# Ten of sixteen decayed sums moved from a matmul to VectorE's scan between two turns, and three weighings of the last pairs moved from TensorE to VectorE

## The chip, the cores and the metric

The kernel runs on one core of a Trainium2 chip. The metric is the device time of one execution in microseconds. The kernel before took 465.46 us (median of three runs, 465.07 to 465.91).

## The reference, cut to what matters

Four gated blocks in a row work on `x`, 32 sequences of 128 tokens with 256 features, with a context `ctx_1024` of the same shape. All arithmetic is in float32. Only the first and the end of the last are touched by the change.

```python
# block 1: a decayed sum of the squared context, times the normed x
def _L0_xattn_ref(q, k, v):            # q = layernorm(x), k = v = ctx_1024
    kv = swapaxes(k * v, 0, 1)
    def step(r, kv_t):
        r = 0.9 * r + kv_t             # along the 128 tokens of a sequence
        return (r, r)
    _, rs = jax.lax.scan(step, r0, kv)
    return q * swapaxes(rs, 0, 1)

x = x + tanh(g_xattn[0]) * _L0_xattn_ref(layernorm(x), ctx_1024, ctx_1024)
x = x + tanh(g_ffn[0])   * _L0_ffn_ref(layernorm(x), ...)       # dense layer and a gated low-rank one
x = x + tanh(g_xattn[1]) * _L1_xattn_ref(layernorm(x), ctx_1024, ctx_1024, mask, ...)  # sigmoid attention, 16 heads
x = x + tanh(g_ffn[1])   * _L1_ffn_ref(layernorm(x), ...)       # 8 experts, the two best for each token
```

In the last block each token gets two rows back from its two experts, each weighed by its gate, and both are added to `x`.

## The kernel before

The 32 sequences go through in 16 **pairs** `p` (tiles of 128 tokens x 2 sequences x 256 features). After the first three blocks the pairs are gathered in four **units** (4, 4, 5 and 3 pairs) for routing: each token's row is sent to a table `xs` in HBM by an indirect DMA on POOL's queue (`send`, L1133), sorted by expert. Then 36 expert **blocks** `i` are worked: 19 early ones of 256 rows, whose rows come from the first three units, and 17 late ones of two halves of 128 rows, which wait for the last unit's sends. A block is fetched on SP's queue (`fetch_x`, L1482 and L1486), turned on TensorE (L1493), multiplied twice (L1538, L1564), and its rows are put to a table `ys` in HBM by indirect DMAs on POOL (`put`, L1587). At the end (`result`, L1760) each pair gathers its rows with `get_y` on SP (L1709), adds them to `x` and stores on ScalarE's queue (L1756).

**Order.** A planner (`Plan`, L109) takes well over a thousand jobs, each with an engine, a cost in ns, what it comes after, what buffer rings it takes and when it gives them back, and a rank; `LATER` (L81) shifts the rank of each kind of job. `settle` plays them through, one queue per engine, and `emit` writes out every engine's instructions in that order. The engines then work through their queues in order and wait by semaphores. The 16 pairs are at many stages at once, so that TensorE's queue mixes products of several pairs, and of expert blocks from the third unit on. PSUM gives four banks of one ring `ps`, and two double ones for attention scores.

**A pair's first block.** `load_pair` (L274) fetches context and x on SP; the context has six places (ring `c`), given back after `scan`. `turn0` (L679) turns the context by four 128x128 transposes on TensorE into a PSUM bank; `keep0` (L683, ScalarE, L685) copies the turned context to SBUF for the products k (L874) and v (L903). `kv` (L689) squares the unturned context in place on ScalarE (L690). `scan` (L703) is one matmul with a 128x128 matrix `decay` of powers of 0.9, already multiplied by tanh of the gate (L447), over 512 columns (L705). `gated_a` and `gated_b` (L711, L723, VectorE) multiply by x less its mean and by `root0` (one over the deviation, POOL, L627 and L628), and add to x.

**Further on in a pair** come `turn1` and `small` (L672, L747), `base` (L839, L848), `norm2` on POOL (L660) and `turn2`, q (L874) with its two copies `qz0` (VectorE, L893) and `qz1` (ScalarE, L895), scores `sc` (L928, four products of 32 rows side by side), tanh on ScalarE (L938), `av` (L953, four products of 32 columns side by side), its copy (VectorE, L967), `o` (L974) and its add to x (`added`, L977).

**The result phase.** For pairs 0 to 9 VectorE adds with two multiply-adds per sequence, 256 wide (L1723). From pair 10 on (`WEIGHED`) it is TensorE: ScalarE writes diagonal matrices of the gates (`gates_of`, L1741), `weigh` (L1743, L1746) is two matmuls per sequence that sum both weighed rows in a PSUM bank of ring `ps`, and VectorE adds that to x (L1720).

```python
job("turn0", "PE", 440, turn0, ["load", ("first",)], kv="k v", ps="keep0")
job("kv", "ACT", 600, kv, ["turn0"])
job("scan", "PE", 860, scan, ["kv", ("decay",)], g="gated_b", ps="gated_a")
```

Here a name after the engine and cost is the function, the list is what the job comes after, and `ps="gated_a"` says that it takes a bank until `gated_a` is done.

Of the kernel before, what the change touches and what calls it, by code (L numbers as in the profile page):

```python
# [10 lines left out]
AF = mybir.ActivationFunctionType  # L11
ALU = mybir.AluOpType
# [3 lines left out]
P = 128  # L16
B, S, D = 32, 128, 256
NC = D // P
NH, HD = 16, 16
GB = 4  # L20
TP = 2
NP = B // TP
UNITS = (4, 4, 5, 3)
NU = len(UNITS)
FIRST = [sum(UNITS[:u]) for u in range(NU + 1)]
UNIT = [u for u in range(NU) for _ in range(UNITS[u])]
NTM = TP * max(UNITS)
E1, RMAX = 4, 8
PROJ = 64
# [6 lines left out]
DECAY = 0.9  # L36
# [26 lines left out]
def done_by(u):  # L63
# [9 lines left out]
DONE = [done_by(u) for u in range(NU)]  # L73

WEIGHED = 10
FILLS = 8


LANDED = (4500, 7000, 10500, 13000)

LATER = {  # L81
    "inputs": 3, "wk": -2, "wv": -0.5, "wq": 4, "first": 0.25, "ones": 0.25, "decay": 2.25,
    "sim_a": -2.75, "sim_b": -1, "sim_c": 3, "sim_d": 1.5, "sim_f": -3, "crw_b": -2, "rwa": -1.25,
    "wb_s": -2.25, "wb_t": -3.25, "wb_k": -1, "wb_m": 1.25, "wb_p": -0.5, "wu_t": 1, "wu_k": 1.5,
    "wu_m": 1.25, "wu_p": 0.5, "wo_s": 3.5, "wo_t": -0.25, "wo_k": -0.75, "wo_m": 2.25,
    "wo_p": -0.75, "cff_a": -0.25, "cff_b": 1.25, "pads": -0.75, "zeros": 2.25, "numbers": -4,
    "lay": 0.5, "lay_bias": 4, "lay_inner": -2, "load": 3.5, "turn0": -2.25, "keep0": 1,
    "stats0": -2.75, "kv": 2.25, "scan": -0.75, "gated_a": -3.75, "mean1": 1.5, "turn1": 0.75,
    "keep1": -1.25, "squares1": 2.5, "root1": -1.25, "small_p": 1, "keep_small": 0.75,
    "keep_logits": -1.25, "small_n": -0.25, "small_q": -2.75, "best_a": -0.25, "best_t": 0.25,  # L90
    "best_b": 3.75, "up_t": -2, "keep_up": -0.75, "base": 3.75, "based": 0.25, "mean2": -4,
    "squares2": 1.75, "root2": 0.75, "norm2": 0.25, "turn2": -4, "k": 1, "q": 2.25, "qz0": -0.25,
    "qz1": 3.75, "sc0": -2, "pr01": -0.25, "v": 4, "vp0": -0.5, "sc1": -1, "pr10": -1.5,
    "pr11": -0.5, "av0": 3.75, "keep_av0": 0.25, "keep_av1": -4, "o0": -3.25, "o1": -3.25,
    "added1": 0.25, "mean3": -3, "squares3": 4, "root3": -1.75, "best": 4, "tanh": -1.75,
    "second": 0.5, "count": 1.5, "places": 0.75, "begun": -2.25, "handing": 3.75, "placed": -2.75,
    "label": -1.75, "send": 4, "settled": 2.25, "hand": -0.25, "weights": 3.25, "weights2": -1.25,
    "last tanh": 0.25, "last second": 1, "last count": -2.5, "last begun": -1.25,
    "last first": -0.75, "last label": -0.5, "last settled": -0.75, "last hand": 3,
    "last weights": -1.75, "last weights2": 0.75, "early_a": -0.5, "early_p": 4, "early_t": -1,  # L100
    "early_c": -1.25, "early_d": -1, "early_o": -0.75, "late_a": -2.5, "late_p": -0.5,
    "late_b": -1.25, "late_t": 1.75, "late_c": 2, "fetch_x": 3.5, "turn_b": -4, "keep_b": -3.25,
    "dest": -4, "inner": -1.5, "outer": 4, "keep_y": -0.5, "put1": 1.75, "copy_w0": 1,
    "copy_w1": 0.25, "get_y": 0.5, "add_y0": 0.5, "add_y1": 0.5, "store": 1.5, "gates": 3,
    "weigh0": -2.75, "weigh1": 2,
}


# [116 lines left out]
def gated_blocks_kernel(ctx: ExitStack, tc: tile.TileContext, a: dict, out: bass.AP):  # L225
# [15 lines left out]
    def ctile(shape, name, dtype=F32):  # L241
        return const.tile(shape, dtype, tag=name, name=name)

    def bank(name):
        return ps1.tile([P, 512], F32, tag="ps", name=name)
# [36 lines left out]

    gates, decay = ctile([P, 4], "gates_sb"), ctile([P, P], "decay_sb")
    temp, sim = ctile([P, 1], "temp_sb"), ctile([PROJ, E1], "sim_sb")
    wp, bp_col = ctile([PROJ, D], "Wp_sb"), ctile([PROJ, P], "bp_col_sb")
    wff = ctile([P, NC, NFF], "wff")
    wbase, wsmall = wff[:, :, 0:XW], wff[:, :, XW:NFF]
    biasb = ctile([P, NSL], "biasb")
# [77 lines left out]
    def numbers():  # L366
        def iota_f(t, pattern, mult=0):
            ti = small.tile(list(t.shape), I32, tag="iota", name=t.name + "_i", bufs=1)
            nc.gpsimd.iota(ti, pattern=pattern, base=0, channel_multiplier=mult)
            nc.gpsimd.tensor_copy(t, ti)  # L370

        iota_f(tok2, [[2 * P, B]], 2)
        iota_f(nth, [[1, 2 * LATE]])
        iota_f(rank, [[1, 1]], 1)
        nc.gpsimd.tensor_scalar_mul(moved, rank, -float(BLK))
        nc.gpsimd.tensor_scalar_add(short, rank, -float(NBLK))
        for t in (held, blocks, shift, handed):
            nc.gpsimd.memset(t, 0.0)

    def counts():  # L380
        nc.gpsimd.memset(below, 0.0)
# [47 lines left out]
    def setup():  # L429
        order = iter(range(1000))  # L430

        def job(what, eng, ns, fn, after=(), ps=None, rank=-1, at=0):
            takes = [("ps", ((ps,),))] if ps else []
            if what.endswith("_t"):
                takes.append(("x1T", ((what[:-1] + "m",),)))
            plan.add((what,), eng, ns, fn, [(x,) for x in after], takes, (rank, next(order)), at)
# [161 lines left out]
        job("zeros", "POOL", 600, zeros, rank=2.2)  # L598
        job("numbers", "POOL", 1300, numbers, rank=2.2)
        job("counts", "POOL", 700, counts, rank=2.2)  # L600
        for k in range(FILLS):
            job(f"fill{k}", "SP", 4000, lambda k=k: fill(k), ["zeros"], None, 4.5 + 0.5 * k, 60000)
        for e in range(E2):
# [78 lines left out]

    def keep0(p):  # L683
        t = work.tile([P, NC, TP * P], F32, tag="kv", name=f"cT_sb_{p}", bufs=4)
        nc.scalar.copy(t.rearrange("p c t -> p (c t)"), st[p].pop("cTp"))  # L685
        st[p]["cT"] = t


    def kv(p):  # L689
        nc.scalar.activation(c_t[p], c_t[p], AF.Square)  # L690

    def stats0(p):
# [6 lines left out]

    def root0(p):  # L700
        root_of("n0", p, st[p]["mv"][:, :, 1], 1.0, ALU.add, EPS)

    def scan(p):  # L703
        pr = st[p]["scan"] = bank(f"scan_{p}")
# [521 lines left out]
    def pair(p):  # L1226
# [15 lines left out]
            job("load", "SP", 0, lambda p: None, at=LANDED[p] - 4200, c="scan")  # L1242
        else:
            job("load", "SP", 950, load_pair, [("load", 3)], c="scan")
        job("turn0", "PE", 440, turn0, ["load", ("first",)], kv="k v", ps="keep0")
        job("keep0", "ACT", 590, keep0, ["turn0"])
        job("stats0", "DVE", 900, stats0, ["load"], mv="gated_a root0")
        job("root0", "POOL", 900, root0, ["stats0", ("first",)], ro0="gated_b")
        job("kv", "ACT", 600, kv, ["turn0"])
        job("scan", "PE", 860, scan, ["kv", ("decay",)], g="gated_b", ps="gated_a")  # L1250
        job("gated_a", "DVE", 790, gated_a, ["scan", "stats0"])
        job("gated_b", "DVE", 950, gated_b, ["gated_a", "root0"])
        job("mean1", "POOL", 225, lambda p: mean_of("n1", p), ["gated_b"], nm1="squares1")
# [441 lines left out]
    def y2_ring(p):  # L1695
        return Y2[p % len(Y2)]

    def get_y(p):
# [14 lines left out]
        if u < NU - 1:  # L1713

            apart(got, f"got{u}", f"put{u}")

    def add_y(p, j):
        b = p * TP + j
        if p >= WEIGHED:
            nc.vector.tensor_add(x_t[p][:, j, 0:D], st[p].pop(("wy", j)), x_t[p][:, j, 0:D])  # L1720
            return
        for k in range(2):
            nc.vector.scalar_tensor_tensor(  # L1723
                x_t[p][:, j, 0:D],
                st[p]["y2"][:, j, k, :],
                gate[:, k, b : b + 1],
                x_t[p][:, j, 0:D],
                ALU.mult,
                ALU.add,
            )  # L1730

    def gates_of(p):

        t = work.tile([P, TP, ROW], F32, tag="row", name=f"gates_{p}", bufs=6)
        t = st[p]["gates"] = t.rearrange("p j f -> p (j f)")[:, 0 : 4 * P].rearrange(
            "p (j k t) -> p j k t", j=TP, k=2
        )
        for j in range(TP):
            for k in range(2):
                b = p * TP + j  # L1740
                nc.scalar.activation(t[:, j, k], ident, AF.Copy, scale=gate[:, k, b : b + 1])  # L1741
# [18 lines left out]
    def result(p):  # L1760
        def job(what, eng, ns, fn, after, **takes):
            plan.add(
                (what, p),
                eng,
                ns,
                fn,
                after,
                [(r, tuple((x, p) for x in until.split())) for r, until in takes.items()],
                (200 + p,),
            )  # L1770

        u = UNIT[p]
        puts = [(f"put{h}", "b", i) for i in range(DONE[u]) for h in range(2)]
        gates = [("weights2", "u", u), ("norm3", p)]
        if p < WEIGHED:
            job("get_y", "SP", 800, lambda: get_y(p), puts, **{y2_ring(p): "add_y0 add_y1"})
            for j in range(TP):
                job(f"add_y{j}", "DVE", 990, lambda j=j: add_y(p, j), [("get_y", p)] + gates)
        else:
            sent = [x for u in range(NU) for x in sends([u])]  # L1780
            job("gates", "ACT", 1000, lambda: gates_of(p), gates + sent, row="weigh0 weigh1")
            job("get_y", "SP", 800, lambda: get_y(p), puts, **{y2_ring(p): "weigh0 weigh1"})
            for j in range(TP):
                job(f"weigh{j}", "PE", 880, lambda j=j: weigh(p, j), [("get_y", p), ("gates", p)], ps=f"add_y{j}")
                job(f"add_y{j}", "DVE", 450, lambda j=j: add_y(p, j), [(f"weigh{j}", p)])
        job("store", "ACT", 450, lambda: store(p), [("add_y0", p), ("add_y1", p)])

    plan.add(("inputs",), "SP", 0, inputs, rank=(-2,))
# [95 lines left out]
```

## Time and profile before

| what | value |
| --- | --- |
| time, median of 3 (range) | 465.46 us (465.07 to 465.91) |
| the profiled execution, its time | 465.25 us |
| its span | 463.4 us (1.85 us lie around it) |
| mean granted TensorE clock | 0.991 |
| DMA | 66.69 MB, mean 144 GB/s |

The page gives the busy time of each engine: PE is TensorE's matmuls, PEld its weight loads, DVE VectorE, ACT ScalarE, POOL GpSimd, SP the engine that issues most DMAs. In a list of groups a row has line, engine, operation, output and inputs, shapes and count, then busy us and mean ns of one, then the idle time just before and what ended it. In a timeline a row begins with start and length in us; what stands in brackets is idle time before it and who ended it. A matmul in float32 can show as two records (the scan's 16 matmuls show as 32), and records overlap, so a matmul's price in a full queue is from its start to the next one's.

### The profile page before, as it was taken

To read this page: it belongs to the slowest core of one execution; us is meant where nothing else is said; L and a number is where in the kernel's file an instruction comes from. 1 tells how busy PE (TensorE), PEld (TensorE's weight loads), DVE (VectorE), ACT (ScalarE), POOL (GpSimd) and SP (SyncE) were. 2 spreads that over 40 slices of the span, in tenths; PEclk is the share of its full clock that TensorE was granted. 3 is DMA by queue.
4 is the path that set the end of the run, shared out by engine and by line. 5 is a ranking of instruction groups with operands and counts; after the bars stand their busy time and mean duration, and the time that the engine had idled before them with its cause. 6 is when DMAs were issued, how large, how long until landed. Compare 5 with 4: busy or idle time off the path is not lost.

```text
span 463.4 us, 10947 instructions
## 1 busy us (share of the span) xinstructions
PE 446.6 (96%) x3594; PEld 366.7 (79%) x3594; DVE 267.5 (58%) x1079; ACT 281.5 (61%) x690; POOL 273.5 (59%) x498
## 2 busy tenths in 40 slices
PE   4999999999999999999999999999999999999966
PEld 3787777877877777878677877788888899999955
DVE  4688554574977455887646286548642232225882
ACT  3666668667666675766685575755443797666400
POOL 7475522643578873488861357887777755454530
PEclk9999999999999999999999999999999999999987
DMA  6936999811823110022430003533665374449976
GB/s 172 321 117 185 232 231 231 177 47 34 287 93 91 59 36 18 8 90 83 132 88 24 1 3 103 161 116 113 188 198 154 123 221 138 127 143 353 365 264 229
DMA packets 53448, 66.69 MB, mean 144 GB/s; under 512 B 6541, under 2 KB 45070, under 8 KB 53264
## 3 DMA queue, kind: packets, MB, share of 16 engines
q1 hardware_dynamic: 41680, 44.60, 35.8%
q0 software_dynamic: 6528, 16.86, 10.0%
q10 hardware_dynamic: 5184, 4.53, 2.9%
q8 instruction: 29, 0.48, 0.4%
q14 instruction: 27, 0.22, 0.2%
HBM read 34.36 MB, written 32.65 MB: 145 GB/s over the span
## 4 chain that ended last, share of the span: by engine, by line
PE 87%; POOL 4%; DVE 3%; ACT 2%; issue 2%; DMA 1%; SPq 0%; POOLq 0%; DVEq 0%
PE ph L1538 14%; PE y L1564 13%; PE sc L928 7%; PE q L874 6%; PE av L953 6%; PE o L974 6%; PE v L903 5%; PE ff L839 5%; PE k L874 5%; PE xbT L1493 3%; PE scan L705 3%; PE sl L747 3%; PE wy L1746 2%; PE ff L848 2%; PE cT L672 2%
## 5 line engine op out<-in xcount | busy, mean ns | idle before, releaser
L1587 POOL DMA_INDIRECT ys<-yb,dsti x72 | 70.4, 977 | 45.6 <-DVE yb L1579 23.5
L1133 POOL DMA_INDIRECT xs<-row,r2pi x64 | 65.9, 1029 | 17.9 <-issue 14.8
L938 ACT ACTIVATE pr<-sc 128x1024 f32<-128x1024 f32 x64 | 61.8, 1017 | 17.4 <-PE sc L928 17.3
L1538 PE MATMUL ph<-xT,w 128*128 128x128 f32 (+1 forms) x424 | 68.3, 313 | 0.0
L1564 PE MATMUL y<-w_outer,ge 128*128 x288 | 66.6, 379 | 0.0
L1552 ACT ACTIVATE ge<-ph,bias 128x128 f32<-128x128 f32 (+1 forms) x106 | 35.4, 405 | 49.8 <-PE ph L1538 48.5
L646 ACT ACTIVATE sq_n<-x,nm_n 128x256 f32<-128x256 f32 x96 | 48.8, 508 | 25.3 <-POOL nm_n L634 23.2
L1538 PEld LDWEIGHTS ph<-xT,w 128*128 128x128 f32 x424 | 60.0, 191 | 3.8 <-issue 0.2
L1564 PEld LDWEIGHTS y<-w_outer,ge 128*128 128x128 f32 x288 | 53.0, 190 | 6.3
L1579 DVE TENSOR_TENSOR yb<-y,b_out_sb 128x256 f32<-128x256 f32 (+1 forms) x53 | 25.8, 516 | 48.5 <-PE y L1564 48.4
L628 POOL TENSOR_TENSOR ro_n<-va_n,half 128x2 f32<-128x2 f32 x64 | 46.2, 722 | 5.3
L928 PE MATMUL sc<-qz,kT 32*128 32x256 f32 x512 | 40.3, 398 | 1.3 <-ACT qz L895 1.3
L953 PE MATMUL av<-pr,vpad 128*32 128x129 f32 x1024 | 34.4, 276 | 0.0
L974 PE MATMUL o<-Wo_sb,avT 128*128 128x265 f32 x128 | 34.2, 392 | 0.0
L953 PEld LDWEIGHTS av<-pr,vpad 128*32 128x32 f32 x1024 | 26.6, 109 | 8.6 <-issue 4.7
L928 PEld LDWEIGHTS sc<-qz,kT 32*128 32x128 f32 x512 | 26.3, 184 | 8.6 <-issue 2.4
L839 PE MATMUL ff<-wff,x1T_sb 128*128 128x265 f32 x128 | 32.1, 393 | 0.0
L634 POOL TENSOR_SCALAR nm_n<-x 128x2 f32<-128x2 f32 x48 | 11.5, 239 | 33.7 <-DVE x L977 20.0
L874 PE MATMUL q<-xT_sb,Wq_sb 128*128 128x256 f32 x128 | 31.2, 386 | 0.0
L903 PE MATMUL v<-Wv_sb,cT_sb 128*128 128x256 f32 x128 | 30.7, 383 | 0.0
L874 PE MATMUL k<-cT_sb,Wk_sb 128*128 128x256 f32 x128 | 30.5, 381 | 0.0
L627 POOL TENSOR_SCALAR va_n<-rs_qn 128x2 f32<-128x2 f32 x48 | 9.7, 201 | 34.8 <-ACT sq_n L646 33.1
(273 smaller groups left out, 858.8 us busy)
## 6 DMA issues: line engine op xcount, KB each, us to landing
xs<-w_outer SPq DMA_DIRECT2D x8, 1290.0 KB, 22.1
xb<-xs SPq DMA_DIRECT2D x19, 258.0 KB, 3.2
xb<-xs SPq DMA_DIRECT2D x34, 129.0 KB, 2.6
w_inner<-in_ctx_dram SPq DMA_DIRECT2D x16, 256.0 KB, 5.2
x<-in_x_dram SPq DMA_DIRECT2D x16, 256.0 KB, 4.8
y<-ys SPq DMA_DIRECT2D x8, 512.0 KB, 7.4
pr<-ys SPq DMA_DIRECT2D x8, 512.0 KB, 8.0
out_dram<-x ACTq DMA_DIRECT2D x16, 256.0 KB, 6.3
```

The lines of the kernel that those rows point to most:

```text
L646: nc.scalar.activation(sq, x_t[p][:, j, 0:D], AF.Square, bias=col(means[k, p], j), accum_out=acc[:, j : j + 1],)
L839: nc.tensor.matmul(pbs[j], xT[:, c, j * P : (j + 1) * P], wbase[:, c, :], start=(c == 0), stop=False,)
L874: nc.tensor.matmul(pk[:, m, :], w[:, c, m * P : (m + 1) * P], st[p][src][:, c, :], start=(c == 0), stop=(c == NC - 1),)
L903: nc.tensor.matmul(pv[:, j, :], st[p]["cT"][:, c, j * P : (j + 1) * P], wv[:, c, :], start=(c == 0), stop=(c == NC - 1),)
L928: nc.tensor.matmul(scs[rp][:, i, m * 2 * P : (m + 1) * 2 * P], kT[r0 : r0 + 32, m, j * P : (j + 1) * P], qz[r0 : r0 + 32, m, j].rearrange( ...
L938: nc.scalar.activation(prs[2 * j + rp][:, :, :, 0:P], st[p]["sc", j][rp].rearrange("p i (w t) -> p i w t", w=4), AF.Tanh, scale=0.5,)
L953: nc.tensor.matmul(av[32 * r : 32 * r + 32, m, :], vp[:, w0 : w0 + 32], prs[2 * j + r // 2][:, r % 2, 2 * m + q, :], start=(q == 0), stop= ...
L974: nc.tensor.matmul(po, avT[:, m, :], wo[:, m, :], start=(m == 0), stop=(m == NC - 1))
L1133: sent = nc.gpsimd.indirect_dma_start(out=xs, out_offset=bass.IndirectOffsetOnAxis(ap=v["pi"][:, k, i : i + 1], axis=0), in_=st[FIRST[u] + ...
L1538: nc.tensor.matmul(ph[:, m, k * n : (k + 1) * n], w[:, c, m * P : (m + 1) * P], bs[i]["xT"][:, c, k * n : (k + 1) * n], start=(c == 0), st ...
L1564: nc.tensor.matmul(py[:, h, :], bs[i]["ge"][:, m, h * P : (h + 1) * P], w_outer[:, bass.ds(ex[h % len(ex)], 1), m].rearrange("p e f -> p ( ...
L1587: sent = nc.gpsimd.indirect_dma_start(out=ys, out_offset=bass.IndirectOffsetOnAxis(ap=bs[i]["dsti"][:, h : h + 1], axis=0), in_=bs[i]["yb" ...
```

## The change

For pairs 6 to 15 (`SCANNED = 6`) the decayed sum is no longer a matmul. ScalarE squares the **turned** context out of PSUM into the context's place (features on partitions, tokens along the free axis); VectorE's scan runs twice over 256 elements (two sequences of 128 tokens side by side; the rate tile `keeps` is 0.9, and 0 at a sequence's first token); four transposes turn the sums back into a PSUM bank. The gate's tanh, which the matrix held, is multiplied into `root0` by one more POOL instruction. The bank of the turned context is given back after `keep0` and `kv`, not after `keep0` alone. `keeps` takes the place of `Wp_sb`, which is widened to 128 partitions, and is filled by two POOL memsets after `sim_e`.

In the last unit (pairs 13 to 15) the first of the two sequences, j = 0, is added by VectorE with two multiply-adds; its two matmuls and its two gate matrices fall away. All values of `LATER` are replaced.

```diff
+SCANNED = 6
 LATER = {
-    "inputs": 3, "wk": -2, "wv": -0.5, "wq": 4, "first": 0.25, "ones": 0.25, "decay": 2.25,
...
+    "wk": -1.75, "wv": 0.5, "wq": -0.75, "first": -1.25, "ones": -2, "tg": -0.25, "sim_a": 3.5,
...
+    def keep_rates():
+        nc.gpsimd.memset(keeps, DECAY)
+        nc.gpsimd.memset(keeps.rearrange("p (j t) -> p j t", t=P)[:, :, 0:1], 0.0)
...
+        job("keeps", "POOL", 700, keep_rates, ["sim_e"], rank=2.3)
...
+    def summed(p):
+        for c in range(NC):
+            t = c_t[p][:, c]
+            nc.vector.tensor_tensor_scan(t, keeps, t, 0.0, ALU.mult, ALU.add)
+
+    def turn_s(p):
+        pr = st[p]["scan"] = bank(f"scan_{p}")
+        t = c_t[p].rearrange("p j d -> p (j d)")
+        for c in range(NC):
+            for j in range(TP):
+                nc.tensor.transpose(
+                    pr[:, j * D + c * P : j * D + (c + 1) * P],
+                    t[:, (c * TP + j) * P : (c * TP + j + 1) * P],
+                    ident,
+                )
+
     def kv(p):
+        if p >= SCANNED:
+            nc.scalar.activation(
+                c_t[p].rearrange("p j d -> p (j d)"), st[p]["cTp"], AF.Square
+            )
+            return
         nc.scalar.activation(c_t[p], c_t[p], AF.Square)
...
     def root0(p):
         root_of("n0", p, st[p]["mv"][:, :, 1], 1.0, ALU.add, EPS)
+        if p >= SCANNED:
+            nc.gpsimd.tensor_scalar_mul(roots["n0", p], roots["n0", p], tg[:, 0:1])
...
-        job("turn0", "PE", 440, turn0, ["load", ("first",)], kv="k v", ps="keep0")
+        job("turn0", "PE", 440, turn0, ["load", ("first",)], kv="k v", ps="keep0 kv")
...
-        job("scan", "PE", 860, scan, ["kv", ("decay",)], g="gated_b", ps="gated_a")
+        if p >= SCANNED:
+            job("summed", "DVE", 950, summed, ["kv", ("keeps",)])
+            job("scan", "PE", 440, turn_s, ["summed"], g="gated_b", ps="gated_a")
+        else:
+            job("scan", "PE", 860, scan, ["kv", ("decay",)], g="gated_b", ps="gated_a")
...
+    def weighed(p, j):
+        return p >= WEIGHED and not (UNIT[p] == NU - 1 and j == 0)
+
     def add_y(p, j):
         b = p * TP + j
-        if p >= WEIGHED:
+        if weighed(p, j):
...
-        for j in range(TP):
+        for j in [j for j in range(TP) if weighed(p, j)]:
             for k in range(2):
                 b = p * TP + j
                 nc.scalar.activation(t[:, j, k], ident, AF.Copy, scale=gate[:, k, b : b + 1])
...
+                if weighed(p, j):
+                    job(f"weigh{j}", "PE", 880, lambda j=j: weigh(p, j), [("get_y", p), ("gates", p)], ps=f"add_y{j}")
+                    job(f"add_y{j}", "DVE", 450, lambda j=j: add_y(p, j), [(f"weigh{j}", p)])
+                else:
+                    job(f"add_y{j}", "DVE", 990, lambda j=j: add_y(p, j), [("get_y", p)] + gates)
```

## The prediction

> **What bounds the kernel now.** I read the share of busy time and the chain that ended last first, on the page of the profile.
>
> ```profile
> PE 446.6 (96%) x3594; PEld 366.7 (79%) x3594; DVE 267.5 (58%) x1079; ACT 281.5 (61%) x690; POOL 273.5 (59%) x498
> ...
> PE 87%; POOL 4%; DVE 3%; ACT 2%; issue 2%; DMA 1%; SPq 0%; POOLq 0%; DVEq 0%
> ```
>
> TensorE is busy 446.6 of 463.4 us and carries 87% of the chain; every other engine has some 40% free. A busy share is an average, so I then read stretches. From 60 to 441.8 us TensorE stands still for about 2 us in all. Its 16.8 us of idle time lie at the start (5.8 us up to 20 us), around 40 to 60 us (1.1), and at the end (4.1 us in one wait, 0.6 later, 3.2 for the last store). So in the long middle, TensorE time removed comes off the end, unless a wait fills the hole. The last 20 us are another stage:
>
> ```profile
> 441.80:449.60 7.80, 3.66 (x17) 2.87 (x16) 7.50 (x19) 0.00 (x0) 3.15 (x4) 0.93 0.63 210
> 449.60:460.20 10.60, 9.98 (x32) 7.98 (x32) 4.34 (x11) 0.00 (x0) 0.00 (x0) 0.73 0.79 284
> ```
>
> (Stretch, length, then busy us of PE, PEld, DVE, ACT, POOL; granted clock; DMA share; GB/s.) First VectorE is full and TensorE waits, then TensorE is full at a mean clock of 0.73. The page's execution took 465.25 us: span 463.4 and 1.85 around it. It stands 0.21 below the median 465.46; I sum against 465.25.
>
> **1. The scan of pairs 6 to 15.** Per pair one matmul of 512 columns goes, and four 128x128 transposes come.
>
> ```profile
> 97.73 1.02 PE L705 MATMUL scan<-w_inner,decay_sb 128*128 128x512 f32 x2
> 98.59 1.89 PE L903 MATMUL v<-Wv_sb,cT_sb 128*128 128x256 f32 x8
> ...
> 102.09 0.60 PE L672 MATMUL cT<-ident,w_inner 128*128 128x128 f32 x4
> 102.53 1.89 PE L874 MATMUL k<-cT_sb,Wk_sb 128*128 128x256 f32 x8
> ```
>
> Records overlap, so the price is start to start: scan 98.59 - 97.73 = 0.86 us, four transposes 102.53 - 102.09 = 0.44. That is -0.42 a pair, ten pairs **-4.2 us**. Bounds: after an operation that uses part of the array the same pieces take longer (x1T 0.59 after av, scan 0.97 after sc), so 0.27 to 0.53 a pair, -2.7 to -5.3.
> [...] Here a record does last 273 ns, but the next starts after 0.11, and the granted clock is 1.00 in every stretch from 0 to 441.8 with three such groups per pair in it; I go by the row.
>
> What comes beside it: VectorE gets 20 scans of 128x256. No row has that size; these are nearest.
>
> ```profile
> L1076 DVE TENSOR_TENSOR_SCAN r2run<-seg,cnt x4: 245/274/308, 123.0 to 315.8; 128x64 f32<-128x64 f32 x2, 128x80 f32<-128x80 f32 x1, 128x48 f32<-128x48 f32 x1
> ...
> L723 DVE SCALAR_TENSOR_TENSOR x<-g,ro_n,x 128x256 f32<-128x256 f32 x32 | 14.2, 482 | 0.0
> ```
>
> Between 48 and 80 elements a scan grows by 63 ns in 32, 1.97 ns each; 256 elements give 0.308 + 176 x 0.00197 = 0.65 us. The lower end is the row of the same size, 0.48; the upper end twice that, 0.96. I take 0.65, as it comes from the same operation: 1.3 us a pair, 13 us in all on an engine with 37 us free of 120 between 120 and 240 us.
> [...]
>
> Does the new path hold TensorE up? It runs turn0, Square on ScalarE (0.64, L690; first in its queue now, the copy after it, so the PSUM bank is held 0.64 longer), two scans, turn back. With 0.15 us of hand-over at each step the first half is ready 1.7 us after turn0, the second 2.35. In the order issued, the TensorE work between is 4 us or more for pairs 6, 9, 10, 13, 14 and 15, and some 3 us for 11; but for 7, 8 and 12 only two output products of 0.9 and a turn of 0.44, 2.24 us. There I expect 0.2 to 0.3 us of wait each. Behind the scans in VectorE's queue stand the adds of o (which free PSUM banks) and qz, late by up to 0.35 a pair against plan. **+1.0 us**, bounds 0 and +4 (0.4 for each pair).
> Hidden at no cost: ten POOL multiplies of 128x2 (0.2 each, L627; POOL is 72% busy there) and two memsets; Square from PSUM instead of SBUF (0.59 against 0.64, like L685); six gates copies fewer on ScalarE (0.4 each).
>
> **2. The order.** All ranks change, so every queue is resorted; the last 17 blocks and the result phase keep their order. On TensorE, entries to and exits from the partial-array forms (sc, av) fall from 115 to 109, at 0.1 to 0.2 us: **-0.6** (0 to -1). At the start pn moves behind scan_1 (TensorE waited 0.47 for it at 10.5 us) and Square comes before the copy, so scan_1 starts at about 10.1 instead of 10.94: **-0.5** (0 to -1). The first turn still waits for its load at 3.8 us. Waits elsewhere are not to be told from before's trace; bounds -1 and +3, value nil.
>
> **3. The end.** Three of twelve weighings (0.87 us each at full clock) go from TensorE; VectorE does two multiply-adds instead of one add.
>
> ```profile
> 443.63 5.59 DVE L1723 SCALAR_TENSOR_TENSOR x<-y,gate,x 128x256 f32<-128x256 f32 x12
> ...
> 449.60 5.49 PE L1746 MATMUL wy<-pr,gates 128*128 128x256 f32 x12 [4.14 <-DVE x L1720]
> 451.71 0.42 DVE L1720 TENSOR_TENSOR x<-wy,x 128x256 f32<-128x256 f32 x1 [1.17 <-PE wy L1746]
> 453.42 0.43 DVE L1720 TENSOR_TENSOR x<-wy,x 128x256 f32<-128x256 f32 x1 [1.28 <-PE wy L1746]
> ...
> 459.69 0.43 DVE L1720 TENSOR_TENSOR x<-wy,x 128x256 f32<-128x256 f32 x1 [0.51 <-PE wy L1746]
> 460.15 0.38 ACTq L1756 DMA_DIRECT2D out_dram<-x  x1
> ```
>
> Up to 449.2 nothing changes: the twelve multiply-adds of pairs 7 to 9 bind. Pair 10's weighings are swapped and its adds not, so the first bank comes free one add (0.35) later: TensorE goes on at 449.95. Five weighings are left instead of eight. Three run slow (before's adds behind them come at 451.71, 453.42 and 455.13, 1.71 apart), two faster (about 1.0), so their results are there at 453.8 (pair 12 whole), 455.5, 456.5, 457.5. VectorE: adds of 12 to 454.6; pairs 13 and 14, j=0, four multiply-adds of 0.445 to 456.4; two adds to 457.1; pair 15, two multiply-adds to 458.0 and one add to 458.4. Before it was 460.1: **-1.7**. VectorE is now late, not TensorE, so the three weighings do not bring their 2.6. Bounds: -2.6 (TensorE alone) and 0 (if the last gather of ys, issued at 448.0 and taking up to 8.8 us, or the stores' queue set the end).
>
> Sum: -4.2 - 0.6 - 0.5 - 1.7 + 1.0 = -6.0, so 465.25 - 6.0 = **459.3 us**.
>
> **Rivals.** (a) The gain of the middle is given back to POOL (8%). Its queue is full from the third unit's sends to the last one's, and the first late block is fetched right behind:
>
> ```profile
> 281.03 1.13 POOL L1133 DMA_INDIRECT xs<-row,r2pi  x1 [1.54 <-DVE r2pi L1117]
> ...
> 364.75 0.99 POOL L1133 DMA_INDIRECT xs<-row,r2pi  x1 [0.30 <-issue]
> ...
> 367.40 8.92 SPq L1486 DMA_DIRECT2D xb<-xs  x10
> ...
> 370.51 0.52 DVE L1519 SCALAR_TENSOR_TENSOR dsti<-xb,exp_f 128x1 int32<-128x1 f32 x2
> ...
> 371.20 0.60 PE L1493 MATMUL xbT<-ident,xb 128*128 128x128 f32 x4
> ```
>
> The slack is only some 0.5 us. If that queue did not start earlier, the 4.3 gained before 371 would shrink to 0.5, with 1.7 at the end: 463.0. Against it: the third unit's count is issued 10 us of TensorE work earlier, between it and that turn there are 97.8 us of matmuls instead of 93.8, and POOL has two puts fewer (-2.6) and one norm more (+2.3) in between, so slack grows to about 4.
>
> (b) The waits behind VectorE's scans take the upper bound (12%): +4 instead of +1, 462.3.
>
> (c) Slower (8%): one mechanism, VectorE's queue in order from pair 6 to 15. A scan waits for a Square that waits in ScalarE's queue, and the adds of o and qz behind it wait with it, until TensorE has no PSUM bank or no qz. From 0.70 us of new TensorE idle time a pair (7.0 over ten) the gain is gone; at the whole 1.3 us of the scans it is -7.0 + 13 = +6, 471.3; at 1.0 a pair, 468.3. For it: before's TensorE already waits twice for a qz (1.3 us in all). Against it: most pairs have more than 2.35 us of cover.
>
> (d) The edit does not do what it says (within 0.2%, 5%): the new order's waits (+3), the scans' (+4) and no gain at the end (+1.7) instead of +1.0 and -1.7 come together: about 465.
>
> **Chances.** Forecast (457.2 to 461.5) 67%; (a) 8%; (b) 12%; (d) 5%; (c) 8%. A measurement here tells about 0.2% (0.9 us) from no change. Faster 0.87, same 0.05, slower 0.08. The range, 457.0 to 463.6, holds the forecast, (a) and (b).
>
> **What would show it.** Right: TensorE busy about 440 us; turn-back groups 0.44 from start to start; a scan of 256 elements near 0.65; idle time of TensorE from 60 to 440 us at 2 to 4 us; at the end TensorE done a microsecond before VectorE. Wrong: waits of TensorE for VectorE's w_inner over 3 us; idle time before the first late turn of xb; the last adds later than 9.5 us after the first weighing that waited.

## The result, and the profile after

The changed kernel takes **472.52 us** (median of 5 runs, 472.26 to 473.93) beside 465.07 for the earlier one on the same chip (5 runs): ratio 1.0159, 95% interval 1.014 to 1.0178. It is 1.6% slower; the forecast was 459.3, the range 457.0 to 463.6. The profiled execution took 472.52 us, its span is 470.7. Experiments 5 to 18 ran where the earlier kernel itself took 486 to 496 us, so each of them is read only as a ratio to the earlier kernel's runs beside it.

The line of busy times of the page, after:

```profile
PE 444.7 (94%) x3602; PEld 365.8 (78%) x3602; DVE 277.4 (59%) x1102; ACT 279.7 (59%) x684; POOL 279.9 (59%) x510
```

VectorE has 9.9 us more than before, POOL 6.4 (twelve instructions more), TensorE only 1.9 less, where some 7 less had been forecast. The stretches say where its idle time is (length, then busy us of PE, PEld, DVE, ACT, POOL):

```profile
20.00:60.00 40.00, 36.74 (x213) 29.09 (x213) 28.38 (x135) 23.27 (x71) 24.67 (x62) 1.00 0.66 175
...
140.00:240.00 100.00, 94.22 (x930) 74.62 (x921) 69.52 (x287) 64.74 (x161) 74.74 (x134) 1.00 0.21 68
```

The same stretches before:

```profile
20.00:60.00 40.00, 38.94 (x262) 31.10 (x261) 30.61 (x138) 26.13 (x77) 21.38 (x51) 1.00 0.76 194
...
140.00:240.00 100.00, 98.06 (x920) 76.87 (x916) 65.84 (x283) 66.99 (x168) 73.22 (x138) 1.00 0.22 69
```

TensorE is busy 2.2 and 3.8 us less there. From 340 us to the end of the blocks nothing differs.

The two pieces that were worked out by hand came as forecast. The source line of the scan (min, median, max in ns; below it who waited for it) and two neighbours in TensorE's timeline:

```profile
L699 DVE TENSOR_TENSOR_SCAN w_inner<-Wp_sb,w_inner x20: 655/675/901, 77.5 to 228.9; 128x256 f32<-128x256 f32 x20
...
  PEld scan L706: 0.2, 1
```

```profile
146.42 0.60 PE L706 MATMUL scan<-ident,w_inner 128*128 128x128 f32 x4
146.86 1.89 PE L904 MATMUL k<-cT_sb,Wk_sb 128*128 128x256 f32 x8
```

The scan takes 0.675 us (0.65 forecast), the turn back 0.44 from start to start, and TensorE almost never waits for it (0.2 us in all). Yet the kernel is slower, so the loss lies elsewhere.

**How the loss is counted.** Busy time hides short waits, because records overlap: the turn above lasts 0.60 us, and the next product begins after 0.44. So I priced every group of matmuls in TensorE's order by its pitch in a full queue, start to start in the profiles (0.43 us for a pass of 512 columns, 0.216 for 256, 0.1085 for a turned 128x128 and so on), set the sum against the time at which the group starts, and took off the median cost of a change of form (0.07 to 0.19 us). What is left is waiting; it comes out 0.1 to 0.2 us above the idle time that the waits of the profile show for the same place. In us, from one profile each:

| us of the span | before | 2: end alone | 1: new order, TensorE's sums | after | 3: old order followed | 4: old ranks |
|---|---|---|---|---|---|---|
| 0 to 20 | 7.2 | 6.4 | 5.4 | 8.5 | 6.7 | 7.4 |
| 20 to 60 | 2.1 | 2.1 | 4.7 | 5.2 | 3.1 | 3.1 |
| 60 to 120 | 1.0 | 1.0 | -0.1 | 0.2 | 3.4 | 1.4 |
| 120 to 180 | 2.0 | 1.9 | 2.1 | 2.4 | 6.5 | 7.5 |
| 180 to 240 | 1.0 | 1.0 | 0.7 | 6.5 | 6.1 | 3.4 |
| 240 to 300 | 0.8 | 0.8 | 4.0 | 4.5 | 1.7 | 1.6 |
| 300 to 340 | 0.0 | 0.0 | 0.7 | 0.6 | 0.2 | 9.1 |
| 20 to 340 | 6.9 | 6.9 | 12.1 | 19.4 | 21.0 | 26.1 |

Before against after: waits +12.5 from 20 to 340 us and +1.3 before, TensorE's work -4.2 for the sums, changes of form -0.7 (14.9 to 14.2), the end -1.8: together +7.1, and the span grew by 7.3. In the columns 3 and 4 the waits include stretches at a lower granted clock (0.98 from 140 to 240 us in 3; 0.97 there and from 240 to 340 in 4).

### The profile page after: what moved, and what is told of

Same layout as the page of the kernel before. It is cut to its first block, busy times and chain, and to the rows that moved or that the text cites. A ratio compares the mean times of both kernels' runs of the same rounds, so it can differ in the third digit from the quotient of the medians.

```text
span 470.7 us, 11016 instructions
## 1 busy us (share of the span) xinstructions
PE 444.7 (94%) x3602; PEld 365.8 (78%) x3602; DVE 277.4 (59%) x1102; ACT 279.7 (59%) x684; POOL 279.9 (59%) x510
## 5 line engine op out<-in xcount | busy, mean ns | idle before, releaser
L1504 ACT COPY w<-w_inner 128x512 f32 x49 | 29.1, 635 | 0.1
```

## The experiments

Theory A said that the new order of all ranks loses the time; theory B that the path of the scans does.

**1, the new order with TensorE's sums.** Every queue keeps the changed kernel's order, and the bank of the turned context is still held until `keep0` and `kv` are done.

```diff
     def summed(p):
-            nc.vector.tensor_tensor_scan(t, keeps, t, 0.0, ALU.mult, ALU.add)
+            pass
     def turn_s(p):
-        ...
+        scan(p)
     def kv(p):
-        if p >= SCANNED: ...
     def root0(p):
-        if p >= SCANNED: ...
```

> The changed kernel's order of instructions is kept as it is on every engine, but the sums of pairs 6 to 15 are TensorE's one matmul again (no scans on VectorE, no turn back, no extra multiply on POOL); the end stays changed. Theory A (the new order of all ranks loses the time, the scans cost what the prediction priced): the idle time of TensorE stays near the changed kernel's 11.1 us between 20 and 340 us, the matmuls cost 4.2 us more, so 472.5 + 2 to 4 = 474 to 477 us. Theory B (the scans' path and VectorE's longer queue hold TensorE up): idle time from 20 to 340 us falls to the earlier kernel's 3 us, so 472.5 - 8 + 4 = 467 to 469 us.

468.16 us, ratio 1.0048 (1.0029 to 1.0067): between the earlier and the changed kernel, on B's side. With 4.2 us more of TensorE work it is 5.2 faster than the changed kernel (1.0159 - 1.0048 = 0.0111 of 465.5). Waits from 20 to 340 us fall from 19.4 to 12.1. So in one and the same order, the path of the scans makes 7.3 us of waits in these two profiles, 3.1 net of the 4.2 that it saves. The 5.2 of the medians isn't all from there: of the 6.5 us between the two profiled spans, some 3 arise in the first 20 us, where TensorE's slow start lasts longer (last section), and no run shows whether the scans have a part in that.

**2, the end alone.**

```diff
-SCANNED = 6
+SCANNED = NP
-LATER = {the new ranks}
+LATER = {the earlier ranks}
-        job("keeps", "POOL", 700, keep_rates, ["sim_e"], rank=2.3)
-        job("turn0", ..., ps="keep0 kv")
+        job("turn0", ..., ps="keep0")
```

> The earlier kernel with its ranks and its matmul scans; only the end is changed (the first tiles of pairs 13 to 15 added by VectorE). Both theories: -1.8 us, from VectorE's first multiply-add of the late stage to the end 17.9 us instead of 19.8, so 463.3 to 463.9. If the end brings nothing by itself, 465.1 and the 1.8 us seen in the changed kernel's last stage come from elsewhere.

462.89 us, 0.9934 (0.9912 to 0.9956), the fastest kernel of this study, faster than both and a little under the 463.3 expected. VectorE's first multiply-add of the late stage to the end is 17.4 us (443.03 to 460.4) instead of 19.8. Against it, experiment 1 prices the new order: the same sums and the same end, 1.0048 - 0.9934 = 0.0114, 5.3 us. So A has its half too. Two waits of the order are easy to see in experiment 1, and experiment 2 has neither of them:

```profile
PE scan L719 <- ACT w_inner L704: 1.9, 1, 1.9
PE sc L942 <- DVE qz L907: 0.9, 1, 0.9
```

The first stands ahead of the scan of pair 4, put right behind two turns, the second ahead of a score product. The changed kernel has both (1.7 and 0.9 us).

**3, the earlier order followed.** The plan is made twice: with the earlier jobs and ranks, then with the changed jobs, each ranked by its earlier start.

```diff
-    plan.settle()
+    plan.settle(old)
+    was = dict(plan.start)
+    for n, j in plan.jobs.items():
+        ...
+        j[5] = (was[n] if n in was else was["kv", n[1]] + 600) / 1000
+    plan.settle(plan.jobs)
```

> Scans on VectorE and the changed end, but the earlier kernel's order: its plan is made first with its own jobs, and each instruction of the changed kernel then takes the rank of its old start; the scans take their place 600 ns behind Square. Theory A: about the prediction without the order's -1.1, so 459 to 462. Theory B: the ten pairs' waits stay, 0.7 us or more a pair, so 467 or more.

473.48 us, 1.0176 (1.0147 to 1.0206). A's forecast fell: the earlier order does not save the scans. With the end changed alike, the scans' path costs 1.0176 - 0.9934 = 0.0242, 11.3 us, in an order that was not made for it. Chain by engine on the page of 2, then one line of its waits (us, times, longest):

```profile
PE 87%; POOL 4%; DVE 3%; ACT 2%; issue 2%; DMA 1%; DVEq 0%; SPq 0%; POOLq 0%
```

```profile
PE xT L679 <- POOL w_inner L667: 1.5, 6, 0.4
```

The same two views of 3:

```profile
PE 68%; POOL 13%; DVE 5%; issue 4%; ACT 2%; DMA 1%; SPq 1%; DVEq 0%; POOLq 0%; ACTq 0%
```

```profile
PE xT L679 <- POOL w_inner L667: 6.1, 10, 1.6
```

POOL goes from 4% to 13% of the chain, 18 to 61 us, and what TensorE waits for most is the norm that POOL writes.

**4, the earlier ranks.** The changed kernel with the earlier table alone.

```diff
-LATER = {the new ranks}
+LATER = {the earlier ranks}
```

> The changed kernel with the earlier kernel's table of ranks put back (the planner sorts the changed jobs anew, so the order is neither kernel's). Theory A: the old ranks are good for this work too or merely unsuited: 460 to 468, idle time of TensorE from 20 to 340 us 4 to 10 us and in other places than in the changed kernel. Theory B: 470 or more, with idle time at the ten pairs' turn back.

478.4 us, 1.0276 (1.0248 to 1.0304): the planner makes of the old ranks a third order, with 9.1 us of waits at 300 to 340 us. It tells how much hangs on the order, and neither theory from the other: B's number came, but not its place, as no wait of TensorE for a turned sum is among those of the profile.

**Where the scans' path makes TensorE late.** Experiment 1 and the changed kernel issue the same instructions in the same order on each engine, but for the sums and multiplies themselves, so each other instruction has a partner, and the difference of the two starts is its lateness. At 55 us TensorE, VectorE and POOL have +3.7 to +3.8, nearly all of it from the start (last section). TensorE then gains 0.42 to 0.47 at each turn back: +2.4 at 113 us, +2.2 at 162. That is the -4.2 of the prediction, seen step by step. The others follow, except in one stretch. TensorE's waits from 140 to 240 us, after:

```profile
PE ff L869 <- DVE x L1007: 1.9, 1, 1.9
PE xT L678 <- POOL w_inner L666: 1.6, 2, 1.1
PE cT L678 <- PE av L983: 0.6, 1, 0.6
...
PE v L933 <- DVE x L882: 0.5, 1, 0.5
```

The same view of experiment 1 has two lines in all:

```profile
PE sc L942 <- ACT qz L909: 0.6, 1, 0.6
PE xT L678 <- POOL w_inner L666: 0.2, 1, 0.2
```

POOL's timeline, after (L731 is the new multiply by the gate's factor):

```profile
171.74 0.69 POOL L634 TENSOR_TENSOR ro_n<-va_n,half 128x2 f32<-128x2 f32 x1
172.54 0.28 POOL L731 TENSOR_SCALAR ro_n<-ro_n,tg 128x2 f32<-128x2 f32 x1
172.91 0.19 POOL L633 TENSOR_SCALAR va_n<-rs_qn 128x2 f32<-128x2 f32 x1
...
175.31 0.22 POOL L640 TENSOR_SCALAR nm_n<-x 128x2 f32<-128x2 f32 x1
```

and the partners in experiment 1:

```profile
168.25 0.70 POOL L634 TENSOR_TENSOR ro_n<-va_n,half 128x2 f32<-128x2 f32 x1
169.03 0.19 POOL L633 TENSOR_SCALAR va_n<-rs_qn 128x2 f32<-128x2 f32 x1
...
171.02 0.22 POOL L640 TENSOR_SCALAR nm_n<-x 128x2 f32<-128x2 f32 x1
```

POOL's lateness is 3.49, then 3.88 behind one multiply, and 4.29 behind the next (at 175.06): 0.4 each, 0.28 of work and 0.1 of issue. Only these two of the ten multiplies fall here; the other eight run from 28.9 to 120.5 us. From 132 to 175 us POOL's lateness grows by 1.9 us, and the two multiplies are 0.8 of that. The rest is four instructions that take 0.2 to 0.4 us longer than their partners, at 131.94, 142.50, 143.38 and 159.58 us, less 0.4 won back at 150. All four run beside a scan. From 157 to 175 us POOL never waits for anyone; it sends the rows of a unit, one in 1.3 us, and roots and means stand between. TensorE meanwhile is at +2.16. The 2.1 us between them come out as waits: ScalarE's squares wait for the mean of 175.31, its tanh of the scores stands behind the squares, av behind these, and so on.

```profile
180.32 0.63 PE L678 MATMUL cT<-ident,w_inner 128*128 128x128 f32 x4 [0.58 <-PE av L983]
...
182.92 0.33 PE L678 MATMUL xT<-ident,w_inner 128*128 128x128 f32 x1 [1.07 <-POOL w_inner L666]
```

The norm for which the two halves of this turn wait is written by two POOL instructions that run beside the scans of pair 12 (181.90 to 183.41 us). After, then their partners in experiment 1:

```profile
181.84 1.93 POOL L666 TENSOR_SCALAR w_inner<-x,nm_n,ro_n 128x256 f32<-128x256 f32 x2
```

```profile
177.57 1.10 POOL L666 TENSOR_SCALAR w_inner<-x,nm_n,ro_n 128x256 f32<-128x256 f32 x2
```

With the turn of xT split in two and the o behind it, these steps lose 3.0 us, and TensorE is at +5.1 at 184 us, later than POOL was at 175.

The second place is at 228 us. VectorE, then POOL, after:

```profile
228.34 1.25 DVE L699 TENSOR_TENSOR_SCAN w_inner<-Wp_sb,w_inner 128x256 f32<-128x256 f32 x2
```

```profile
228.67 1.76 POOL L790 COPY x<-sl 128x16 f32<-128x16 f32 x1
```

The partner in experiment 1:

```profile
223.44 0.21 POOL L774 COPY x<-sl 128x16 f32<-128x16 f32 x1
```

A copy of 128x16 takes 1.76 us instead of 0.21. It starts during the two scans and ends (230.43) as the two multiply-adds behind them end (230.38). By what mechanism it is held is not shown. POOL's lateness goes from +5.2 to +6.8 there, and the roots that VectorE needs come that much later:

```profile
236.80 0.17 DVE L821 TENSOR_TENSOR r_d<-sm,ro_ss 128x8 f32<-128x8 f32 x1 [3.15 <-POOL ro_ss L634]
...
237.28 0.77 DVE L1007 TENSOR_TENSOR x<-o,x 128x265 f32<-128x265 f32 x2
```

The adds of o stand behind the waiting r_d in VectorE's queue, they free the bank that ff of pair 12 needs, and TensorE loses 2.0 us. A wait of 0.7 us at 153.8 (base behind the same kind of chain) is the third. Together 5.7 of the 7.3 us.

I call this theory P: POOL's queue is the pace of the second and third units' sends; TensorE's gain only carries it up to POOL, and POOL itself became longer, 279.9 us against 273.6. The ten multiplies are 2.9 of that. Sixteen POOL instructions overlap a scan, and nine of these take 0.2 to 1.6 us longer than their partners, 4.7 us in all, more than the multiplies; others take somewhat less. Not every long one is a scan's: in experiment 1 a send beside VectorE's multiply-adds takes 1.57 us (at 223.81).

**5 to 18, taking parts of the path away.** They were to tell VectorE's load (C), the longer chain (D) and POOL's multiplies (E) apart. All use the new order but 7.

5, 10, 14, 16 and 18: no scans (pairs 6 to 15 are left unsummed).

```diff
     def summed(p):
-            nc.vector.tensor_tensor_scan(t, keeps, t, 0.0, ALU.mult, ALU.add)
+            pass
```

> The changed kernel with its order, but the 20 scans of pairs 6 to 15 are left out (the sums over the context are not computed; what is squared is turned back as it is). Square, turn back and POOL's multiplies stay. Theory C (VectorE's longer queue: 13 us more in an engine that works in order): the waits of TensorE from 20 to 340 us fall to those of the run with TensorE's sums in the new order, so 472.5 - 7 to 9 = 464 to 466. Theory D (the longer chain of pieces, turn, Square, turn back, each waiting for the one before in another engine's queue): only the scans' 1.3 us a pair leaves the chain, 467 to 470.

> The same kernel as the run without scans (the sums over the context of pairs 6 to 15 are not computed; turn, Square, turn back and POOL's multiplies stay). Theory C (VectorE's 13 us): 464 to 466. Theory D (the chain): 467 to 470. Theory E (POOL's multiplies): 470 to 473, as if the scans cost nothing.

> The changed kernel with its order, the 20 scans left out (the sums over the context of pairs 6 to 15 are not computed), the multiplies on POOL kept. Theories C and D (VectorE's 13 us, as a load or as a link of the chain): the four waits gone, 464 to 468. Theory E: the four waits stay, 470 to 473.

> The changed kernel with its order, the 20 scans left out (the sums over the context of pairs 6 to 15 are not computed), turn, Square, turn back and POOL's multiplies kept. If the scans on VectorE make the four waits of TensorE, as a load or as a link of the chain (theories C and D): the four waits gone, 0.990 to 1.003 of the earlier kernel. If POOL's multiplies make them (theory E): the four waits stay, 1.010 to 1.016.

> The changed kernel with its order, the 20 scans left out (the sums over the context of pairs 6 to 15 are not computed), POOL's multiplies kept. Theory P: POOL's copy at 228.7 us takes 0.2 us instead of 1.76, the wait at 237.8 goes (2 us), the waits at 180 to 184 us stay near 3; 469 to 471. If VectorE's load makes all the waits: 464 to 467. If the scans cost nothing: 472 to 473.

Ratios 1.0163 (1.0086 to 1.024), 1.0119 (1.0042 to 1.0197), 1.0102 (1.0026 to 1.0179), 1.0129 (1.0032 to 1.0225), 1.0262 (1.0205 to 1.0319).

8, 9 and 13: no multiplies on POOL (the gate's factor left out; the first part of the diff); 12 and 17: the multiplies on VectorE (both parts).

```diff
     def root0(p):
-        if p >= SCANNED:
-            nc.gpsimd.tensor_scalar_mul(roots["n0", p], roots["n0", p], tg[:, 0:1])
     def gated_b(p):
+        if p >= SCANNED:
+            nc.vector.tensor_scalar_mul(rs, rs, tg[:, 0:1])
```

> The changed kernel with its order, without POOL's ten multiplies of the norms of pairs 6 to 15 by the gate's factor (that factor is left out of the result). Theory E (POOL's queue passes the lateness on, and 0.28 us more a pair stands in it): 469 to 470.5. Theories C and D: 471.5 to 472.5.

> The same kernel as the run without POOL's multiplies (new order, scans on VectorE, the gate's factor of pairs 6 to 15 left out), because the earlier kernel itself took 27 us longer beside that run. Theory E (the ten multiplies in POOL's queue are what makes TensorE late): 1.000 to 1.005 of the earlier kernel, 465 to 468 us, the wait of xT for POOL's norm (1.07 us at 182.9 in the changed kernel) gone and the one for the add of o (1.94 at 237.8) shorter. Theories C and D: 1.013 to 1.016, 471 to 472.5.

> The changed kernel with its order, without POOL's ten multiplies (the gate's factor of pairs 6 to 15 is left out). Theory E (the multiplies in POOL's queue): 465 to 468 us, and the four waits of TensorE that the changed kernel has and its order with matmul sums has not (0.7 us ahead of v at 153.8, 1.3 ahead of cT at 180.3, 1.2 ahead of xT at 182.9, 2.0 ahead of ff at 237.8) gone. Theories C and D: the four waits stay, 471 to 472.5.

> The changed kernel with its order; the ten multiplies of 128x2 go from POOL to VectorE, each just ahead of the multiply-add that reads it, some 0.1 us each. Theory E: as without the factor, plus at most 1 us: 466 to 469. Theories C and D: 472 to 474.

> The changed kernel with its order; the ten multiplies go from POOL to VectorE, 0.1 us each. Theory P (POOL's queue is full from 140 to 240 us; it falls behind by 0.33 to 0.41 us with each multiply and by up to 1.6 us where one of its copies meets VectorE's scans, and TensorE waits for what is behind): the waits at 180 to 184 us shrink from 3.0 to some 1.5 us, the one at 237.8 stays near 2, 470 to 471.5. If POOL's multiplies don't matter: 472 to 473.5. If all the waits are theirs: 466 to 468.

Ratios 1.0013 (0.9974 to 1.0053), 1.013 (1.0049 to 1.0211), 1.0136 (1.0042 to 1.023); 1.0076 (1.0031 to 1.0121), 1.0101 (1.0031 to 1.0171).

6, 11 and 15: experiment 1 with 20 scans over constants; 7: experiment 2 with them.

```diff
     def summed(p):                                   # 6, 11 and 15
+            nc.vector.tensor_tensor_scan(idle, keeps, wq[:, 0], 0.0, ALU.mult, ALU.add)
     def kv(p):                                       # 7, behind each Square of pairs 6 to 15
+        for c in range(NC * (p >= 6)):
+            nc.vector.tensor_tensor_scan(idle, wq[:, 1], wq[:, 0], 0.0, ALU.mult, ALU.add)
```

> The new order with TensorE's matmul sums, and at the places of the scans in VectorE's queue 20 scans of the same size over constants, which wait for nothing and for which nothing waits. Theory C: the load alone does it, 468.2 + 5 to 9 = 473 to 477. Theory D: an idle load costs little, 468 to 470.

> The same kernel as the run with idle scans in the new order (TensorE's matmul sums, no multiplies on POOL, 13 us of scans over constants on VectorE). Theory C: 473 to 477. Theories D and E: 468 to 470, the time of the run without the idle scans.

> The new order with TensorE's matmul sums and 20 scans over constants at the scans' places in VectorE's queue. Theory C (the load alone): the four waits are back, 468.2 + 5 = 473. Theories D and E: none of the four waits, 468 to 469.

> The earlier kernel's order with the changed end only (462.9 before), TensorE's matmul sums, and behind each Square of pairs 6 to 15 two scans over constants in VectorE's queue: 13 us of load that nothing waits for, at places that the plan doesn't know of. Theory C: 462.9 + 6 to 10 = 469 to 473. Theory D: 463 to 465.

Ratios 1.0051 (1.0009 to 1.0092), 1.0087 (1.0053 to 1.012), 1.0149 (1.0071 to 1.0228); 0.9973 (0.9938 to 1.0008).

The times of these fourteen are inconclusive. The ratio of one and the same kernel differs by up to 1.6% from one set of runs to another, more than the effects looked for. Two waits of 8 show why:

```profile
PE y L1596 <- issue: 5.7, 1, 5.7
PE av L981 <- issue: 5.4, 10, 1.0
```

The first stands at 375 us; from 340 to 440 us TensorE is idle for 7.8 to 12.9 us in each of the fourteen profiles, where the earlier and the changed kernel have none, and the granted clock is 0.97 there in 8. From 139 to 175 us it is idle for 3.6 to 5.5 us in the ten profiles of 5, 8 to 10, 12 to 14 and 16 to 18 (1.2 in the changed kernel), in good part for nothing that the profile shows. So the queues meet otherwise than in the changed kernel. The three waits at 180 to 184 us are at most 0.1 us in these ten, whatever was taken away: where there are scans, the two norm instructions of pair 12 now start ahead of them and take 1.09 or 1.10 us, as in experiment 1.

What the profiles do show is what a scan does to POOL. In the five profiles without scans the copy that took 1.76 us takes 0.21 to 0.26. Where the scans stay, it comes ahead of them and takes 0.20 or 0.21, but the second send behind it meets the last of them instead, here in 8:

```profile
234.68 2.22 POOL L1161 DMA_INDIRECT xs<-row,r2pi  x1 [0.30 <-issue]
```

A send takes 0.99 us in the median. This one takes 2.22 or 2.23 us in 8, 9 and 13, and 1.37 and 1.12 in 12 and 17. The wait of ff of pair 12 goes with it: 0.82 or 0.83 us in 8, 9 and 13, nil in 12 and 17, and nil in all five profiles without scans. So this wait goes with the POOL instruction that a scan lengthens, and neither with VectorE's load (12 and 17 have it too) nor with the multiplies (8, 9 and 13 lack them). Its price in the changed kernel (2.0 us) is read from one profile. Taking the scans away never brought the kernel to the earlier one's time (five ratios, 1.010 to 1.026), so VectorE's load as the whole cause (C) finds no support.

## Why the prediction was wrong

- **Scans, TensorE's work, -4.2:** right; 0.44 for a turn back, 0.42 to 0.47 gained per pair. A scan of 0.675 us is near the forecast 0.65.
- **Waits behind scans, +1.0, bounds 0 and +4:** this is the step that failed: +7.3, beyond the upper bound. The term priced a scan by TensorE's wait for its sums and by what stands behind it in VectorE's queue. TensorE waited 0.2 us for turned sums, so the cover of pairs 7, 8 and 12, which I worked out, was not the matter. The 0.15 us of hand-over at each step was an estimate; where a step waited for the one before it, it started 0.03 to 0.05 us behind (the Square at 93.49 us, the scans at 159.51 and 181.90, the turn back at 226.66). POOL stood at nothing, "Hidden at no cost: ten POOL multiplies of 128x2 (0.2 each, L627; POOL is 72% busy there)", and that a scan lengthens POOL's own instructions stood in no term. The runs showed nine of them longer by 4.7 us in all. A multiply takes 0.29 us, and eight of the ten run before 121 us. The 72% is an average; while POOL sends a unit's rows it waits for no one (157 to 175 us), and the two multiplies there cost 0.4 us of lateness each. POOL's chain (mean, squares, root, norm) ends in TensorE's turns.
- **The order, -0.6 and -0.5, waits elsewhere nil, bounds -1 and +3:** changes of form -0.7 and scan_1 at 10.12 us were right; the second step that failed is "Waits elsewhere ... value nil": 5.3 us by experiments 1 and 2, beyond the bound of +3, though experiment 1 runs work for which that order was not made.
- **The end, -1.7:** right in number; -1.8 in the changed kernel (452.76 to 470.7, 17.9 instead of 19.8), -2.4 alone. The path was as forecast in experiment 2 alone, where TensorE is done 0.8 us before VectorE. In the changed kernel its last weighings waited 0.4 us for the last gather and 0.7 for VectorE, so part of the agreement is luck.
- **Rivals:** (a) named the mechanism, POOL's queue taking the gain back, but put it at the first late block, where nothing is lost (0.6 us from 300 to 340), and held that POOL could at most give the gain back; POOL's own queue grew by 6.3 us. (c) had its threshold of 0.70 us a pair met (7.3 over ten), with VectorE's adds behind a waiting instruction as it said, but that instruction waited for POOL, not for a Square. The forecast of 8% for slower was met by a path that (c) had only in part. To call (c) and (a) two rivals was part of the error: the queues of VectorE, ScalarE and POOL form one ring, and each hands its lateness on.

Shown: the scans' path costs 5.2 us net by the medians in its own order (3.1 of it between 20 and 340 us in the profiles) and 11.3 in the earlier one; the new order costs 5.3; the end gains 3; nine of the sixteen POOL instructions beside a scan take longer, 4.7 us in all. Read from profiles and priced by no run: that POOL's queue is the link to TensorE's other waits, and how the 7.3 us divide between its multiplies and its lengthened instructions. Open: whether an order exists in which the scans pay.

## What to carry to other kernels

Before costing a small instruction at nothing because its engine has time free, look at that engine's queue in the stretch where the instruction falls: POOL, 59% busy over the span, waited for no one from 157 to 175 us, and a multiply of 0.28 us there made what stood behind it 0.4 us later. Ask also what the new instruction does to another engine's instructions beside it: here nine POOL instructions beside a scan took 4.7 us longer than their partners. Where two kernels issue the same order, subtract start times partner by partner on every engine: the engine whose lateness jumps first holds the cause, which lists of waits name only at the far end of the chain. Try the parts of a change alone: here the end alone (0.9934) is the version to keep.

## What the runs showed of the hardware

TensorE ran at half rate at the start for a time that differs between profiles of nearly the same schedule. One turn of 128x128 follows the next after 0.21 us there and after 0.11 later, and four take 1.06 us or 0.63. After, then experiment 1:

```profile
11.98 1.06 PE L526 MATMUL wb<-ident,wff 128*128 128x128 f32 x4
```

```profile
11.16 0.63 PE L526 MATMUL wb<-ident,wff 128*128 128x128 f32 x4
```

The full rate came at about 10 us in experiment 1, 14 in experiment 2, 15 before and 18 in the changed kernel; between the first and the last it is worth 3.3 us of the span (the first product k starts at 15.29 and 18.63). One kernel's runs spread as far (466.0 to 469.0 in experiment 1), but that the start is the cause of that spread is not shown. The page prints a granted clock of 1.00 all the while; the trace's record of the clock begins only where the full rate does, at 9.57, 13.98, 15.00 and 18.44 us; so the prediction's "1.00 in every stretch from 0" holds from 15 us on. The four starts of the full rate lie up to 8.9 us apart; what sets them is not shown.
